# A planned four-layer graph kernel: first batch in halves, first weights on another queue, three batches kept on chip, and a reordered tail

## The chip, the core and the metric

The kernel runs on one core of one Trainium2 chip. The time is the device time of one execution in microseconds (us); where several executions were timed, their median is given. The engines are PE (TensorE, the matrix products), DVE (VectorE), ACT (ScalarE), POOL (GpSimd) and SP (SyncE, which here only issues transfers); "PEld" in the profile is the loading of a product's stationary operand, which lies beside PE's products. The core has 16 DMA engines, which all queues share. One profiled execution gives the trace; all times inside it count from the start of its span.

## What is computed

There are 32 batches; `x` is 32 x 512 x 128, `adj` 32 x 512 x 512, symmetric, of zeros and ones with ones on the diagonal, all float32. Four layers of the form x + f(relu(layernorm(x)), adj) follow each other:

```python
def L0(x, mask):                      # masked attention
    v, q, k = relu(x Wv' + bv), relu(x Wq' + bq), relu(x Wk' + bk)
    h = clip((q k') * mask, 0, 9e13) - 9e15 * (1 - mask)
    return softmax(h, axis=2) @ v
def L1(x, A):                         # A_norm = d^-1/2 (A + I) d^-1/2
    dyn = conv1d(x[:, -128:, :])      # the last 128 rows, kernel width 3
    lw = lstm(dyn)                    # 128 steps, state 32 x 128
    return sigmoid((A_norm @ x) @ lw)
def L2(nodes, adj):                   # four times
    src_agg = l2norm(adj, 2) @ (nodes ws + bs)
    dst_agg = l2norm(adj, 1)' @ (nodes wd + bd)
    return tanh([src_agg, nodes wn + bn, dst_agg] wu + bu)
def L3(clip, adj, W, bias, a):
    g = adj @ (clip W') + bias
    return where(g >= 0, g, a * g)
```

The LSTM of layer 1 runs over the last 128 rows of every batch, and its output enters every row of that batch: nothing behind it can start before its last step.

## The kernel before

The function `symmetric` (L792) computes everything for a symmetric `adj`. It also counts violations into a flag `fail`, and a second program, `general`, runs behind a branch on that flag if it isn't zero. All engines read the flag (`counted`, L1671; `read`) and take the branch at the end.

**Who sets the order.** The code doesn't issue instructions where it names them. Each step is recorded with `plan.op` (helpers `PE`, `ACT`, `DVE`, `POOL`, `DMA`), with its engines, a duration as the planner supposes it, a rank, what it reads and writes, and a `gap` until its result may be used. `Plan.run` (L612) then simulates the engines with these durations, always takes the step that can start first, by rank among equals, and writes the instructions out in that order. A lower rank is more urgent: the LSTM's steps have ranks 0 to 127, loads of the head `HEAD`, pass 1 10,000 and up, pass 2 20,000, the rest 30,000. Two constants say how long a less urgent step may keep an awaited LSTM step from its engine: `HOLD` (L538), and `PATIENCE` (L825) for the products of `fold`. Buffers come from pools of named tags with fixed numbers (`BUFS`: 8 of "x", 5 of "y", 4 each of "n0" to "n3" and "inv", 5 of "xn", 8 PSUM banks "mm"); a step that needs a new buffer waits until the planner sees one free.

**Head.** `load` (L947) issues the attention's weights (`w_att`, 192 KB), the bias columns `colb` and a bias row of V (L954) on SP, behind the two halves of the first batch's x and ahead of the second batch's x. ACT begins with an activation on a scrap tile (L938) that makes it load its table. PE runs 20 products on a constant (`warm_up`, L970). Weights of layer 2 are combined beforehand by `fold` (L1019), four times, placed by `FOLD_AT` behind batches of pass 1.

**Pass 1** (`pass_1`, L1151; 0 to 186 us) takes the batches in order. It loads x (256 KB) and the last 128 columns of adj (`al`), normalises (`ln_full`: statistics L1070 on DVE, a power L1080 on POOL, x-hat L1090 or L1093), transposes and applies relu (`ln_t`, into half 1 of the tile `kh`), computes K (L1168, into half 0 of `kh`), Q for the last 128 rows, and V (L1184), then scores (L1201), exponential (L1205), mask (L1206) and output (L1211) for these rows, and from their new values the convolution's input (L1226, L1236). It stores K and the transposed relu (`dkq`, 448 KB), V (`dv`, 258 KB) and the new last rows (`dl`) in HBM.

**LSTM stage** (186 to 503 us). `lstm` (L1249) runs the 128 steps for all batches at once: products of w with the state (f_z, L1263), tanh (L1289), cell (L1295), state (L1309). Each step is a chain through PE, ACT and DVE, and PE has little of its own to do in it. The gaps are filled with `pass_2` (L1321), the attention of the first 384 rows: it loads `dkq` and `dv` back, the rows of `adj` and x again, and computes Q (L1348), scores (L1357), exponential (L1360), mask and output (L1363, L1367, L1369). Further filler is the early sums of layer 1 (`aggregate`, L1479, with the product at L1483).

**Rest** (`rest`, L1501; 503 us to the end) does layer 1's last product, the four rounds of layer 2 (L1592, L1483, L1599, L1603, L1607) and layer 3 for one batch per turn; the turns overlap. Layer 3 of a turn is: new x (L1622), layer norm, the split of relu into two parts whose sum is used in the product (`relu_parts`, in the last turn `relu_first`, L1461, four 128-column pieces, with ACT's L1472 and DVE's L1474), aggregation (L1636 in the last turn), product with W (L1650), and then three steps for the activation with slope a: the negative part on ACT (L1653), the positive part added on DVE (L1654), and minus a times the negative part (L1656). Then the result is stored. In the last turn (31) the steps from L1636 on come in two halves, and the second half is stored by ACT (L1660). Sixteen products on a constant keep PE at work in the last turn.

## Time and profile before

| what | value |
|---|---|
| median of 3 runs | 1282.03 us (1279.73 to 1284.29) |
| profiled execution | 1284.31 us, its span 1282.4 us |
| granted clock of PE | 1.00 as a mean |
| PE busy | 1255.4 us, 98% of the span |
| DVE, ACT, POOL busy | 982.7, 836.9, 399.3 us |
| moved by DMA | 237.15 MB, 185 GB/s over the span |
| LSTM stage | 186.4 us (first f_z) to 503 us |

A page of the profile gives busy time by engine, the shares of the chain that ended last (followed back from the last instruction to what released it), and groups of instructions by line. Other views are answers of the same trace: waits (who waited for whom: total us, times, longest), stretches (busy time of each engine in a time window), the chain piece by piece in order of time (start, length, what), and a timeline (start, length, engine, line, instruction). Matmuls are pipelined and their ends are modelled, so a PE that is shown as busy need not be at its peak rate.

### The profile page before, as it was taken

How to read it: one execution, taken by the hardware profiler on the slowest of the kernel's cores; microseconds unless marked ns; L12 is line 12 of the kernel's file. 1: busy time of each engine (PE TensorE's matmuls, PEld its weight loads, DVE VectorE, ACT ScalarE, POOL GpSimd, SP SyncE). 2: the span in 40 equal slices, each digit the busy share in tenths (PEclk: the TensorE clock that was granted, in tenths of full speed). 3: DMA queues.
4: the chain of work that ended last, by engine and by line, in shares of the span. 5: the costliest groups of instructions: out<-in, count | busy, mean ns of one | idle time of the engine just before them, and what ended most of it. 6: DMA issues, size and time to landing. Idle time of an engine off the chain costs nothing.

```text
span 1282.4 us, 33056 instructions
## 1 busy us (share of the span) xinstructions
PE 1255.4 (98%) x12073; PEld 970.9 (76%) x12074; DVE 982.7 (77%) x3275; ACT 836.9 (65%) x2099; POOL 399.3 (31%) x734
## 2 busy tenths in 40 slices
PE   9999999999999989999999999999999999999997
PEld 6989876666666667777878778787787787877775
DVE  7798969888989879876667677677676776787745
ACT  5566658777867646776567666676676766675433
POOL 4555533232323224332223224223232242232101
PEclk9999999999999999999999999999999999999999
DMA  8888888887868896778367777777777777473211
GB/s 268 265 264 279 280 272 264 263 267 229 269 201 260 249 245 192 161 179 198 85 151 177 155 164 166 147 176 159 152 180 151 175 151 151 98 163 69 50 25 44
DMA packets 316843, 237.15 MB, mean 185 GB/s; under 512 B 151936, under 2 KB 260736, under 8 KB 316672
## 3 DMA queue, kind: packets, MB, share of 16 engines
q1 hardware_dynamic: 299504, 218.04, 62.3%
q0 software_dynamic: 16896, 16.78, 8.4%
q8 instruction: 97, 1.59, 0.5%
q14 instruction: 74, 0.61, 0.2%
q10 hardware_dynamic: 272, 0.13, 0.0%
HBM read 138.68 MB, written 64.75 MB: 159 GB/s over the span
## 4 chain that ended last, share of the span: by engine, by line
PE 83%; DVE 8%; DMA 2%; ACT 2%; POOL 2%; issue 1%; SPq 0%; ACTq 0%; DVEq 0%
PE f_pa L1483 18%; PE f_py L1592 15%; PE f_pa L1603 15%; PE f_pg L1483 7%; PE f_s L1357 4%; PE f_po L1363 3%; PE f_z L1263 3%; PE f_pk L1168 2%; PE f_pv L1184 2%; PE f_p L1650 2%; PE f_pol L1211 2%; PE f_pl L1557 2%; PE f_sl L1201 2%; PE f_pd L1236 2%; DMA f_a<-in_adj_dram 2%
## 5 line engine op out<-in xcount | busy, mean ns | idle before, releaser
L1483 PE MATMUL f_pa<-f_ar,f_y 128*128 128x512 f32 x1024 | 300.6, 430 | 0.4 <-ACT f_y L1448 0.4
L1483 PEld LDWEIGHTS f_pa<-f_ar,f_y 128*128 128x128 f32 x1024 | 189.3, 188 | 75.8 <-issue 40.4
L1592 PE MATMUL f_py<-f_wf,f_n 128*128 128x128 f32 x1280 | 174.1, 275 | 0.0
L1592 PEld LDWEIGHTS f_py<-f_wf,f_n 128*128 128x128 f32 x1280 | 165.1, 191 | 8.6 <-issue 1.0
L1607 ACT ACTIVATE f_n<-f_pa,f_bcol 128x512 f32<-128x512 f32 x128 | 88.1, 688 | 104.4 <-PE f_pa L1603 101.6
L1603 PE MATMUL f_pa<-f_n,f_wf 128*128 128x512 f32 x320 | 153.1, 593 | 0.2 <-DVE f_pa L1599 0.2
L1403 ACT ACTIVATE f_ar<-f_a 128x512 fp32r<-128x512 f32 x224 | 138.8, 622 | 6.4 <-DMA f_a<-in_adj_dram 4.0
L1410 POOL DMA_DIRECT2D f_das<-f_ar x32 | 27.1, 847 | 365.8 <-ACT f_ar L1403 345.2
L1448 ACT CAST f_y<-f_py 128x512 fp32r<-128x512 f32 x128 | 75.3, 589 | 66.9 <-PE f_py L1592 64.2
L1449 DVE TENSOR_TENSOR f_y<-f_py,f_y 128x512 fp32r<-128x512 f32 x128 | 87.9, 688 | 37.4 <-ACT f_y L1448 36.8
L1599 DVE TENSOR_TENSOR f_pa<-f_pa,f_inv 128x512 f32<-128x512 f32 x128 | 87.0, 695 | 33.5 <-PE f_pa L1483 33.4
L1363 PE MATMUL f_po<-f_v,f_e 128*32 128x129 f32 x3072 | 107.2, 273 | 1.9 <-issue 1.9
L1363 PEld LDWEIGHTS f_po<-f_v,f_e 128*32 128x32 f32 x3072 | 90.1, 110 | 20.3 <-issue 17.1
L1357 PE MATMUL f_s<-f_q,f_k 128*32 128x384 f32 x1024 | 99.0, 487 | 0.2 <-ACT f_e L1360 0.2
L1263 PE MATMUL f_z<-f_w,f_seq 128*32 128x128 f32 x2040 | 83.2, 276 | 11.3 <-DVE f_seq L1309 4.1
L1603 PEld LDWEIGHTS f_pa<-f_n,f_wf 128*128 128x128 f32 x320 | 57.4, 190 | 46.0 <-issue 42.0
L1263 PEld LDWEIGHTS f_z<-f_w,f_seq 128*32 128x32 f32 x2040 | 54.2, 109 | 49.1 <-ACT f_e L1360 11.9
L1121 DVE COPY f_hl_d<-f_n 128x1024 uint16<-128x1024 uint16 x26 | 18.1, 694 | 88.8 <-ACT f_n L1607 88.8
L1419 DVE SCALAR_TENSOR_TENSOR f_aT<-f_a,f_aT 128x1024 bf16<-128x1024 f32 (+1 forms) x68 | 76.3, 1155 | 0.1
L1592 PE MATMUL f_py<-f_wf,f_T_c 128*128 128x128 f32 x448 | 72.9, 275 | 0.0
L1483 PE MATMUL f_pg<-f_ar,f_xp_d 128*128 128x512 f32 x248 | 71.6, 412 | 0.0
L1360 ACT ACTIVATE f_e<-f_s 128x384 f32<-128x384 f32 x128 | 61.1, 484 | 15.2 <-PE f_s L1357 8.5
(208 smaller groups left out, 2751.4 us busy)
## 6 DMA issues: line engine op xcount, KB each, us to landing
f_a<-in_adj_dram SPq DMA_DIRECT2D x112, 256.0 KB
f_a<-in_adj_dram SPq DMA_DIRECT2D x28, 1024.0 KB
f_das<-f_ar POOLq DMA_DIRECT2D x32, 512.0 KB, 4.8
f_dkq<-f_kh SPq DMA_DIRECT2D x32, 448.0 KB
f_dv<-f_v SPq DMA_DIRECT2D x32, 258.0 KB
f_v<-f_dv SPq DMA_DIRECT2D x32, 258.0 KB
f_al<-in_adj_dram SPq DMA_DIRECT2D x32, 256.0 KB
f_k<-f_dkq SPq DMA_DIRECT2D x32, 256.0 KB
```

The costliest lines, as they stand in the source:

```text
L1263: nc.tensor.matmul(z.t[part, k, :, :], h, w[:, m : m + 4, part], start=False, stop=True, skip_group_check=True)
L1357: PE(R, t_mm(NR), lambda s=s, j=j: quarters(lambda p: nc.tensor.matmul(s.t[p], keys.t[:, j * P + p.start : j * P + p.stop], q.t, start=Tru ...
L1363: PE(R, t_mm(P), lambda e=e, t=t, j=j: quarters(lambda p: nc.tensor.matmul(po.t[p, t, :], e.t[:, t * P + p.start : t * P + p.stop], v.t[:, ...
L1403: ACT(rank, 0.62, lambda t=t: nc.scalar.activation(ar.t[:, t, :], a.t[:, t, :], AF.Square, accum_out=deg.t[:, t : t + 1]), [(a, t)], [(ar, ...
L1419: nc.vector.scalar_tensor_tensor(flat(aT.t[:, n * k : n * (k + 1), :]), flat(a.t[:, n * k : n * (k + 1), :]), 1.0, flat(aT.t[:, n * k : n ...
L1448: ACT(rank, t_act(N), lambda: nc.scalar.copy(parts.t[:, :, 0, :], src.t), [src], [(parts, 0)])
L1449: DVE(rank, t_dve(N), lambda: nc.vector.tensor_sub(parts.t[:, :, 1, :], src.t, f32(parts.t[:, :, 0, :])), [src, (parts, 0)], [(parts, 1)])
L1483: nc.tensor.matmul(pg.t, parts.t[:, j, k, :], ar.t[:, j, :], start=(k == 0 and j == 0), stop=(k == 1 and j == NT - 1))
L1592: nc.tensor.matmul(py.t[:, j, :], nodes[n].t[:, bass.ts(j, P)], wf[:, W_F[i] + c, 0, :], start=False, stop=(c == nch - 1), skip_group_chec ...
L1599: before = DVE(R, t_dve(N), lambda pa=pa: nc.vector.tensor_mul(pa.t, pa.t, inv_row.t), [inv_row], [pa])
L1603: nc.tensor.matmul(pa.t, wf[:, W_F[i] + c, 1, :], nodes[n].t, start=False, stop=(c == nch - 1), skip_group_check=True)
L1607: ACT(R, 0.57, lambda pa=pa, n=n, i=i: nc.scalar.activation(n.t, pa.t, AF.Tanh, bias=bcol[:, i : i + 1]), [pa], [n])
```

## The change

It has five parts, and moves the order of the instructions on all engines, since the planner plans everything anew.

1. Planner constants: `HOLD` 0.18 to 0.15, `PATIENCE` 0.9 to 1.3, the folds behind the positions 2, 3, 4, 5 of pass 1 instead of 1, 3, 5, 7. (`LEAD = 0.0` and `Q_FIRST = range(0)` leave branches in the code that do nothing.)
2. The three first weights are issued by ACT (`load_beside`), ahead of its table load.
3. Pass 1 takes batches 3 to 31 first and then 0, 1, 2. The batch at position 0 is handled in two halves of 256 rows up to K, and position 1 has its variance sum on DVE ("quick").
4. Batches 0, 1, 2 (`RESIDENT`) are neither stored after pass 1 nor loaded for pass 2: `kh`, `v` and `xc` stay in their buffers.
5. In the tail, the negative part, its addition and the store of turns 29 and 30 are recorded within `relu_first` of turn 31, behind its fourth piece (`put_off`). In every turn the positive part is recorded ahead of the negative one. The flag is read behind the last store instead of behind the last aggregation.

```diff
--- before.py
+++ after.py
@@ -535,7 +535,7 @@
...
-    HOLD = 0.18
+    HOLD = 0.15
...
-    FOLD_AT = (1, 3, 5, 7)
+    FOLD_AT = (2, 3, 4, 5)
...
+    RESIDENT = range(3)
+    FIRST_GAPS = (2.0, 2.8, 3.0, 3.5)
...
-    PATIENCE = 0.9
+    PATIENCE = 1.3
...
-    nc.scalar.activation(table, neg_half[:, 0, 0:1], AF.Exp)
...
-    w_att = load(HEAD + 0.1, 192, w[:, :W_CONV, :], weights[:, :W_CONV, :])
-    w_cols = load(HEAD + 0.2, 5, colb, cols)
-    DMA(HEAD + 0.3, 64, lambda: nc.sync.dma_start(brow[:, BR_V, :], rows[R_V].partition_broadcast(P)), [], [(biases, BR_V)])
+    def load_beside(dst, src, c, gap):
+        return ACT(HEAD, 0.45, lambda: nc.scalar.dma_start(dst, src), [], [c], gap=gap)
+
+    w_att, w_cols = plan.fixed(w), plan.fixed(colb)
+    load_beside(w[:, :W_CONV, :], weights[:, :W_CONV, :], w_att, 3.5)
+    load_beside(colb, cols, w_cols, 3.0)
+    load_beside(brow[:, BR_V, :], rows[R_V].partition_broadcast(P), (biases, BR_V), 3.0)
+    ACT(HEAD, 1.5, lambda: nc.scalar.activation(table, neg_half[:, 0, 0:1], AF.Exp))
     w_conv = load(HEAD + 12, 192, w[:, W_CONV:W_IH, :], weights[:, W_CONV:W_IH, :])
     w_crow = load(HEAD + 12, 64, conv_row, rows[R_CONV].partition_broadcast(P))
...
-    def pass_1(b):
-        R = 10_000 + b * 10
+    staying = {}
+
+    def pass_1(b, pos):
+        R = 10_000 + pos * 10
         xc = new("x", (P, NT, P), f"f_x_{b}")
-        n = 2 if b == 0 else NT
+        n = 2 if pos == 0 else NT
         for at in range(0, NT, n):
             DMA(R, 64 * n, lambda at=at: nc.sync.dma_start(xc.t[:, at : at + n, :], x[b].rearrange("(t p) d -> p t d", p=P)[:, at : at + n, :]), [],
-                [(xc, t) for t in range(at, at + n)] if b == 0 else [xc], gap=2.0 if b == 0 else 4.5 if b < 4 else 3.5)
+                [(xc, t) for t in range(at, at + n)] if pos == 0 else [xc], gap=FIRST_GAPS[pos] if pos < len(FIRST_GAPS) else 3.5)
         al = new("n1", (P, NT, P), f"f_al_{b}")
         DMA(R + 11, 256, lambda: nc.sync.dma_start(al.t, adj[b, :, NR:].rearrange("(t p) i -> p t i", p=P)), [], [al])
-        xn = ln_full(R, xc, f"a{b}", quick=b == 0)
...
         kh = new("y", (P, 2, N), f"f_kh_{b}")
-        turned = ln_t(R, xn, None, f"a{b}", ((kh, 1), lambda: kh.t[:, 1, :]))
...
+        if pos == 0:
+            hs, ks = [], []
+            xn = new("xn", (P, NT, P), f"f_xn_a{b}")
+            for at in range(0, NT, n):
+                tiles = range(at, at + n)
+                part = slice(at * P, (at + n) * P)
+                mv = ln_stats(R, xc, tiles, f"a{b}_{at}")
+                rs = new("rs", (P, NT), f"f_rs_a{b}_{at}")
+                ln_rstd(R, mv, at, at + n, (lambda rs=rs, at=at: rs.t[:, at : at + n], rs), True)
+                for t in tiles:
+                    DVE(R, t_dve(P), lambda t=t, mv=mv, rs=rs: nc.vector.tensor_scalar(
+                        xn.t[:, t, :], xc.t[:, t, :], mv.t[:, t, 0:1], rs.t[:, t : t + 1], OP.subtract, OP.mult), [(xc, t), mv, rs], [(xn, t)])
+                tp = bank(f"f_xt_a{b}_{at}", (P, n, P), whole=False)
+
+                def turn(tp=tp, tiles=tiles):
+                    for k, t in enumerate(tiles):
+                        nc.tensor.matmul(tp.t[:, k, :], xn.t[:, t, :], ident, start=(k == 0), stop=True, is_transpose=True, skip_group_check=True)
+                turned = PE(R, n * T_TR, turn, [(xn, t) for t in tiles], [tp])
+                hs.append((kh, ("h", at)))
+                ks.append((kh, ("k", at)))
+                evict(R, n * P, lambda part=part: kh.t[:, 1, part], lambda tp=tp: flat(tp.t), [tp], hs[-1:], relu=True)
+                project(R, n * P, W_K, C_K, lambda part=part: kh.t[:, 1, part], lambda part=part: kh.t[:, 0, part], hs[-1:], ks[-1:], f"k_{b}_{at}")
+        else:
+            hs, ks = [(kh, 1)], [(kh, 0)]
+            xn = ln_full(R, xc, f"a{b}", quick=pos == 1)
+            turned = ln_t(R, xn, None, f"a{b}", (hs[0], lambda: kh.t[:, 1, :]))
+            project(R, N, W_K, C_K, lambda: kh.t[:, 1, :], lambda: kh.t[:, 0, :], hs, ks, f"k_{b}")
         ql = new("low", (P, P), f"f_ql_{b}")
-        project(R, N, W_K, C_K, lambda: kh.t[:, 1, :], lambda: kh.t[:, 0, :], [(kh, 1)], [(kh, 0)], f"k_{b}")
-        project(R, P, W_Q, C_Q, lambda: kh.t[:, 1, NR:], lambda: ql.t, [(kh, 1)], [ql], f"ql_{b}")
+        project(R, P, W_Q, C_Q, lambda: kh.t[:, 1, NR:], lambda: ql.t, hs[-1:], [ql], f"ql_{b}")
...
-        PE(R, 4 * t_mm(P), values, [(kh, 1), w_att], [pv])
+        PE(R, 4 * t_mm(P), values, hs + [w_att], [pv])
...
-        DMA(R + 5, 448, lambda: nc.sync.dma_start(dkq.t, flat(kh.t)[:, : N + NR]), [kh], [dkq])
-        DMA(R + 5, 258, lambda: nc.sync.dma_start(dv.t, v.t), [v], [dv])
+        if b in RESIDENT:
+            staying[b] = kh, v, xc
+        else:
+            DMA(R + 5, 448, lambda: nc.sync.dma_start(dkq.t, flat(kh.t)[:, : N + NR]), [kh], [dkq])
+            DMA(R + 5, 258, lambda: nc.sync.dma_start(dv.t, v.t), [v], [dv])
...
-        PE(R, 4 * t_mm(P), scores, [(kh, 0), ql], [s])
+        PE(R, 4 * t_mm(P), scores, ks + [ql], [s])
...
-        keys = new("inv", (P, N), f"f_k2_{b}")
-        hT = new("xn", (P, NR), f"f_h2_{b}")
-        v = new("n3", (P, NT, P + 1), f"f_v2_{b}")
-        xc = new("x", (P, NT if whole else L, P), f"f_x2_{b}")
-        DMA(R, 192, lambda: nc.sync.dma_start(hT.t, dkq.t[:, N:]), [dkq], [hT], gap=LANDED)
-        DMA(R, 256, lambda: nc.sync.dma_start(keys.t, dkq.t[:, :N]), [dkq], [keys], gap=LANDED)
+        stays = b in RESIDENT
+        if stays:
+            kh, v, xc = staying[b]
+            keys, keys_of = kh, lambda: kh.t[:, 0, :]
+            hT, h_of = kh, lambda: kh.t[:, 1, :NR]
+        else:
+            keys = new("inv", (P, N), f"f_k2_{b}")
+            hT = new("xn", (P, NR), f"f_h2_{b}")
+            keys_of, h_of = lambda: keys.t, lambda: hT.t
+            v = new("n3", (P, NT, P + 1), f"f_v2_{b}")
+            xc = new("x", (P, NT if whole else L, P), f"f_x2_{b}")
+            DMA(R, 192, lambda: nc.sync.dma_start(hT.t, dkq.t[:, N:]), [dkq], [hT], gap=LANDED)
+            DMA(R, 256, lambda: nc.sync.dma_start(keys.t, dkq.t[:, :N]), [dkq], [keys], gap=LANDED)
...
-        DMA(R, 258, lambda: nc.sync.dma_start(v.t, dv.t), [dv], [v], gap=LANDED)
-        DMA(R, 192, lambda: nc.sync.dma_start(xc.t[:, :L, :], x[b, :NR].rearrange("(t p) d -> p t d", p=P)), [],
-            [(xc, t) for t in range(L)], gap=LANDED)
-        if whole:
+        if not stays:
+            DMA(R, 258, lambda: nc.sync.dma_start(v.t, dv.t), [dv], [v], gap=LANDED)
+            DMA(R, 192, lambda: nc.sync.dma_start(xc.t[:, :L, :], x[b, :NR].rearrange("(t p) d -> p t d", p=P)), [],
+                [(xc, t) for t in range(L)], gap=LANDED)
+        if whole and not stays:
             DMA(R, 64, lambda: nc.sync.dma_start(xc.t[:, L, :], dl.t), [dl], [(xc, L)], gap=LANDED)
...
+        for finish in put_off:
+            finish(parts.parts[0, NT - 1][0], parts.parts[1, NT - 1][0])
...
+        if turn == B - 1:
+            R += 4
...
-                warm_up(R, 0.216, f"f_warm_{k}_{b}", [end4])
+                warm_up(R - 4, 0.216, f"f_warm_{k}_{b}", [end4])
...
-            late.append(agg3)
...
-            ACT(R, t_act(n * P), lambda p3=p3, part=part: nc.scalar.activation(neg.t[:, part, :], p3.t, AF.Relu, scale=-1.0), [p3], [(neg, at)])
             DVE(R, t_dve(n * P), lambda p3=p3, part=part: nc.vector.scalar_tensor_tensor(
                 flat(xc.t[:, part, :]), flat(p3.t), 0.0, flat(xc.t[:, part, :]), OP.max, OP.add), [p3], mine)
-            DVE(R, 0.15 + 0.125 * n, lambda part=part: nc.vector.scalar_tensor_tensor(
-                flat(xc.t[:, part, :]), flat(neg.t[:, part, :]), minus_alpha, flat(xc.t[:, part, :]), OP.mult, OP.add),
-                [(neg, at), w_alpha], mine)
-            if at:
-                ACT(R, 0.5, lambda part=part: nc.scalar.dma_start(out[b].rearrange("(t p) d -> p t d", p=P)[:, part, :], xc.t[:, part, :]),
-                    mine, [], gap=2.0)
+
+            def finish(turned=(), split=(), at=at, p3=p3, part=part, mine=mine):
+                ACT(R, t_act(n * P), lambda: nc.scalar.activation(neg.t[:, part, :], p3.t, AF.Relu, scale=-1.0), [p3], [(neg, at)], after=turned)
+                DVE(R, 0.15 + 0.125 * n, lambda: nc.vector.scalar_tensor_tensor(
+                    flat(xc.t[:, part, :]), flat(neg.t[:, part, :]), minus_alpha, flat(xc.t[:, part, :]), OP.mult, OP.add),
+                    [(neg, at), w_alpha], mine, after=split)
+
+                def store():
+                    return (nc.scalar if at else nc.sync).dma_start(out[b].rearrange("(t p) d -> p t d", p=P)[:, part, :], xc.t[:, part, :])
+                return ACT(R, 0.5, store, mine, [], gap=0.0) if at else DMA(R, 64 * n, store, mine, [], gap=0.0)
+            if turn in (B - 3, B - 2):
+                put_off.append(finish)
             else:
-                DMA(R, 64 * n, lambda part=part: nc.sync.dma_start(out[b].rearrange("(t p) d -> p t d", p=P)[:, part, :], xc.t[:, part, :]),
-                    mine, [])
+                stored = finish()
+            if turn == B - 1:
+                late.append(stored)
...
-        PE(R, 0.1, read, [], [], after=[said] + late)
+        PE(R + 4, 0.1, read, [], [], after=[said] + late)
...
-    for b in range(B):
-        pass_1(b)
+    for pos, b in enumerate([b for b in range(B) if b not in RESIDENT] + list(RESIDENT)):
+        pass_1(b, pos)
         for i, at in enumerate(FOLD_AT):
-            if at == b:
-                fold(i, 10_000 + b * 10)
+            if at == pos:
+                fold(i, 10_000 + pos * 10)
...
```

## The prediction, made before the changed kernel was run

> **What bounds the kernel now.** The page's first lines and its chain shares say which engine sets the end:
>
> ```profile
> span 1282.4 us, 33056 instructions
> PE 1255.4 (98%) x12073; PEld 970.9 (76%) x12074; DVE 982.7 (77%) x3275; ACT 836.9 (65%) x2099; POOL 399.3 (31%) x734
> PE 83%; DVE 8%; DMA 2%; ACT 2%; POOL 2%; issue 1%; SPq 0%; ACTq 0%; DVEq 0%
> ```
>
> TensorE is idle for only 27 us. The change leaves the products of the computation as they are (one is split in two halves), so those 27 us, and whatever "busy" hides, are all there is. The table by stretches (length, busy time and count of PE, PEld, DVE, ACT, POOL, then clock, DMA share, GB/s) says where:
>
> ```profile
> 200.00:250.00 50.00, 46.80 (x1024) 31.70 (x1020) 43.98 (x182) 37.48 (x134) 15.26 (x28) 1.00 0.85 263
> 400.00:500.00 100.00, 93.12 (x1984) 65.59 (x1980) 85.97 (x359) 64.65 (x229) 31.04 (x56) 1.00 0.89 248
> 550.00:1250.00 700.00, 699.62 (x3768) 546.16 (x3767) 496.63 (x1274) 446.84 (x942) 188.65 (x279) 1.00 0.65 141
> 1250.00:1283.00 33.00, 25.81 (x143) 19.30 (x142) 17.63 (x60) 12.39 (x26) 3.54 (x5) 0.97 0.15 43
> ```
>
> From 550 to 1250 nothing can be won. What can move is the head, the LSTM stage (186 to 503) and the tail. PE's waits, and the LSTM's tanh, whose 128 executions date the steps:
>
> ```profile
> PE f_z L1263 <- DVE f_seq L1309: 4.1, 12, 0.9
> PE f_z L1263 <- issue: 3.0, 3, 2.3
> PE f_pq L1348 <- issue: 2.0, 1, 2.0
> PE f_po L1363 <- issue: 1.9, 2, 1.3
> ```
> ```profile
> L1289 ACT ACTIVATE f_th<-f_z x128: 228/251/259, 187.8 to 502.8; 128x96 f32<-128x96 f32 x128
> ```
>
> (502.8 − 187.8)/127 = 2.48 us a step. The ends of matmuls are modelled, so "busy" hides slack; I priced PE's order by undisturbed pieces of the chain: 1.72/4 = 0.43 us a record of 128x512 (the piece at 1246.83), 1.85/8 = 0.23 for the early sums (1248.55), 2.68/24 = 0.11 for 128x128 (1243.26), and 0.22 for eight of the LSTM's tiled ones (distance of their starts). That makes 276 us of work in the 317 of the LSTM stage, so some 40 of slack; about 10 in pass 1 (20 to 186), 7 from 550 to 1250.
>
> **The LSTM stage.** New: HOLD, PATIENCE, three resident batches. PE's order between two tanh gives each step its work; a step of max(2.17, work + 0.05 + 0.30 for each change to tiled products and back), 2.17 being the shortest steps of the trace, sums to 298.9 us for 126 steps against 313.1 measured. Of the 14.2 above it, 11.2 lie in ten stalled steps. In the changed order the 16 starved steps (under 1.4 us of filler) become 11, and the same sum gives 296.9: −2.0. By the same prices, PE has 1.1 us less to do before the LSTM (170.5 → 169.4) and 0.4 less after it (763.4 → 763.0), the stage itself taking in 1.3 more (276.4 → 277.7): −1.5. Together −3.5 if the chip keeps the planner's timing, 0 if it doesn't; I take −2.8, nearer the first, since the sum already follows the chip's steps to 5% (298.9 against 313.1).
>
> The residents drop 3 × (448 + 258) KB of stores and 3 × (192 + 256 + 258 + 192 + 64) KB of loads, about 5 MB of 237. At the 263 GB/s of the first LSTM stretch that is 19 us of transfer time, but beside PE's work; SP issues 20 instructions fewer. No PE wait above names a load, so the value is bounded by 0 and the 3.5 us of the small waits on masks and scores (rinv 1.5, ar 1.3, el 0.9, all partly load-driven). I take −0.7, near zero, since most name DVE or ACT. What hides the stores today is PE's work; without that cover each 706 KB would cost 2.7 us.
>
> Here a rule speaks. The Trainium skill, "Runtime: NRT & Kernel Launch", section Instruction fetch mechanics, has instruction memory refilled in 16 KiB blocks, with the crossing mostly hidden. The rows differ: the three longest "issue" waits (2.3 at 440.9, 2.0 at 475.1, 1.3 at 208.9; 5.5 us) each stand beside a refill of the instruction queue (from 439.5, 474.7, 207.9). By the rule another order changes nothing there; by the rows up to 5.5 us can go, or come as often again. The changed order has 18 PE rows more in 5,670, so refills are as many and only fall elsewhere; I take 0, with ±3.
>
> The order of batches and the fold's places (1, 3, 5, 7 to 2, 3, 4, 5) are the same instructions in another order; their gaps are in the −1.5 above.
>
> **The head.** SyncE issues, one behind another:
>
> ```profile
> 1.75 0.46 SPq L949 DMA_DIRECT2D f_w<-in_weights_dram  x1
> ...
> 2.73 0.43 SPq L954 DMA_DIRECT2D f_brow<-in_rows_dram  x1
> 3.20 0.43 SPq L1156 DMA_DIRECT2D f_x<-in_x_dram  x1
> ```
>
> The three weights now go out on ScalarE at about 0.74 to 2.1, ahead of the table load (1.28 us), which ends at 3.4 instead of 2.0. Behind it on ScalarE stands the first x-hat at 5.85: 2.2 us of cover. On SyncE the second x goes out at 1.75 instead of 3.20. The fold's first 384 KB move behind it, its mask and three more issues, to about 4.2 from 3.68; they landed at 8.76, so near 9.3, and are first used at 11.4: no cost. The Trainium skill, "DMA: Bandwidth & Descriptors", section Issuing engines are not separate DMA queues, says that all engines' transfers share the same 16 and that a second issuer saves only issue time. By that rule at most 1.45 us, and the weights (192 KB, 0.7 us at the page's 268 GB/s of the first slice) now share the engines with the first x, which can land 0 to 0.5 later. The first chain:
>
> ```profile
> 1.19 6.15 PE f_warm L973 x20
> 7.33 0.45 PE f_xt_a L895 x4
> ...
> 7.81 0.61 ACT f_kh L900
> ...
> 8.46 1.12 PE f_pk L1168 x2
> ...
> 9.80 0.91 PE f_pv L1184 x8
> ...
> 13.36 0.71 PE f_pol L1211 x4
> ```
>
> By halves, each of statistics, power (GpSimd, 1.02 us at 4.60 for four columns) and x-hat starts on its own half of x, so both x-hats are there near 6.5. That wins nothing yet: the 20 warm-up products, counted the same in the changed order, keep PE until 7.17, when the first transpose starts. (They also cover an x that lands 0.5 late.) From there: first half of the relu at 7.6 to 8.0 (half of 0.61, plus overhead), first half of K at 8.0, second at 8.5 to 8.95, where K ended at 9.42: −0.45. Values 9.2 to 10.05, scores from 10.05 to 10.95, which before began at 10.86. Then PE waits for the exponential and the mask: exp 11.1 to 11.6, mask to 12.3. Before, PE idled from 12.25 to 13.36 there. In the changed order the next batch, with its x 1.45 earlier, has its transposes (0.45), the fold's (0.33) and its K product (0.86) ahead of f_pol. Its relu comes on ScalarE behind the exp, 11.7 to 12.3, so K runs 12.3 to 13.2 and f_pol starts at 13.2 with 0.86 more behind it: −1.0. By the rule at most −1.45; by the row of the second x (landed 7.73, near 5 afterwards) I would have counted 2.4. I take −1.0, from −1.4 to +0.3 (DVE is 98% busy from 60 to 80, and may give back what PE wins).
>
> **The tail.** VectorE sets when the last aggregation ends:
>
> ```profile
> 1269.87 0.74 DVE L1656 SCALAR_TENSOR_TENSOR f_x<-f_neg,f_minus_alpha,f_x 128x512 f32<-128x512 f32 x1
> 1271.33 0.87 DVE L1474 SCALAR_TENSOR_TENSOR f_xp_d<-f_yr_d,f_rs_d,f_xp_d 128x128 fp32r<-128x128 f32 x3
> 1272.14 0.75 DVE L1656 SCALAR_TENSOR_TENSOR f_x<-f_neg,f_minus_alpha,f_x 128x512 f32<-128x512 f32 x1
> 1272.81 0.34 DVE L1474 SCALAR_TENSOR_TENSOR f_xp_d<-f_yr_d,f_rs_d,f_xp_d 128x128 fp32r<-128x128 f32 x1
> ```
>
> Both L1656 go behind the fourth part, and on ScalarE the negative part of turn 30 (0.60 at 1271.51) no longer stands before its last x-hat (1272.00): the parts end at about 1272.1 instead of 1273.15, −1.0. The two updates (1.5 us) then run to 1273.6 while PE finishes and warms (1273.9 to 1275.0); uncovered they would give it all back. The stores of turns 29 and 30 start some 1.5 later with them, well ahead of the last one at 1277.8. The final chain: the positive part no longer follows the negative one, −0.4; but the flag read (0.48 on ACT at 1275.49, in the shadow of PE's products) now stands behind the last store's issue, and ACT's branch follows it, +0.5. So 0, from −0.5 to +0.5. Tail: −1.0.
>
> **Sum.** −2.8 − 0.7 + 0 − 1.0 − 1.0 = −5.5. Against the profiled execution: span 1282.4 → 1276.9, and with the 1.9 around it (1284.31 − 1282.4) 1278.8. The median of the runs shown lies 2.3 below that execution: 1282.0 − 5.5 = 1276.5.
>
> **Rivals.** (A) As summed: 1276.5, own range 1273.5 to 1279. (B) The stalled steps were artefacts of this order: half of the 11.2 goes too, about 1271. For it: three of ten are refills, which need not recur. Against: nothing in the change aims at them. (C) The packing doesn't do what it says: steps hang on delays that the planner does not see (4.1 us of PE's waits are on DVE's f_seq), and the 1.3 us of work taken in lengthen the stage. Then 1282.0 − 1.0 − 1.0 − (1.5 − 1.3) = 1279.8. Against: starved steps cost 2.17 whatever they hold. (D) Slower: at the border of the passes the residents hold 3 of 4 buffers "n3" (v) and 3 of 5 "y", so the loads of v for batches 4 to 6 wait for pass 2 of batches 0 to 2. A batch of pass 2 takes 317/32 = 9.9 us, a 256 KB load some 4.5 (x in the head), so one batch of lead suffices; it decides once the loads take over 9.9 us from the freeing, as with DMA at 0.85 busy they might. Then filler is missing for up to two steps a batch: 2 × (2.17 − 0.43 of LSTM products) = 3.5, times three = 10.4, less the 5.5: 1286.9. Two late batches of the three make it slower than before.
>
> **Chances and range.** A 0.50, B 0.20, C 0.20, D 0.10. A measurement of this kernel tells 0.3% (3.9 us) from no change: bounds 1278.2 and 1285.9. Faster: 0.92 of A, all of B, a third of C = 0.73, with a bit of D's low end 0.75; slower: six tenths of D = 0.06; same 0.19. Range 1268.5 (B with all stalls gone but packing halved) to 1282.5 (C with head and tail lost): it leaves out D and a little of B.
>
> **What would show it.** Head: transposes still at 7.2, K's first half near 8.0, scores near 10.1. LSTM: tanh from about 185.6 to 498.5, 2.46 a step; a sum of issue waits near 5 to 7. Border: no PE wait on a v or x load near 185 to 220. Tail: last part of L1527 near 1 us earlier against the n4 transpose, the last branch as far behind the store as before. Wrong if issue waits grow past 10 us, if pass 1 ends no earlier, or if PE waits for v.

## The result and the profile after

The changed kernel took 1276.24 us in the median of ten runs (1274.55 to 1280.98), the kernel before 1283.10 in ten (1279.31 to 1287.63): a ratio of 0.9949, 95% interval 0.9932 to 0.9966, so 6.5 us faster. 5.5 us were forecast. The sum came out nearly right and most of its terms did not, as the traces show. The profiled execution after is one of the shorter ones (span 1273.4, time 1275.34), that of before one of the longer (1284.31); the difference of 9.0 us between those two spans is 2 to 3 us too large. So where I compare stages below I use several traces of the same plan.

The page's first lines and chain shares of the changed kernel:

```profile
span 1273.4 us, 33089 instructions
PE 1255.8 (99%) x12074; PEld 970.9 (76%) x12075; DVE 985.9 (77%) x3275; ACT 837.8 (66%) x2102; POOL 400.7 (31%) x734
PE 86%; DVE 6%; POOL 2%; ACT 2%; DMA 2%; issue 1%; SPq 0%; ACTq 0%; DVEq 0%
```

PE's busy time is the same within 0.4 us; what changed is its idle time, 27 us before and 17.6 after. By stretches (the same columns as before):

```profile
200.00:250.00 50.00, 49.44 (x1088) 34.32 (x1084) 46.49 (x194) 38.35 (x136) 15.37 (x28) 1.00 0.70 218
400.00:500.00 100.00, 97.80 (x1968) 69.69 (x1960) 89.30 (x369) 68.23 (x239) 33.83 (x64) 1.00 0.85 238
550.00:1250.00 700.00, 699.58 (x3763) 545.78 (x3763) 498.08 (x1268) 438.62 (x918) 182.51 (x271) 1.00 0.63 138
```

PE is at work 49.4 us of the first 50 behind 200 (46.8 before) and 97.8 of the 100 from 400 (93.1 before; in the changed kernel the last 8 of them lie behind the LSTM stage); 550 to 1250 has nothing in it, as said. The DMA share at the beginning of the stage fell from 0.85 to 0.70. PE's waits in the stage and the tanh that dates the steps:

```profile
PE f_z L1303 <- DVE f_seq L1349: 2.3, 7, 0.6
PE f_z L1303 <- issue: 0.7, 2, 0.4
PE f_z L1303 <- DVE f_rinv L1419: 0.6, 2, 0.4
PE f_z L1303 <- ACT f_ar L1456: 0.3, 1, 0.3
PE f_s L1409 <- issue: 0.2, 1, 0.2
```
```profile
L1329 ACT ACTIVATE f_th<-f_z x128: 227/251/255, 186.5 to 491.6; 128x96 f32<-128x96 f32 x128
```

Two lines of before that belong beside these:

```profile
PE f_z L1263 <- DVE f_rinv L1367: 1.5, 3, 1.0
PE f_z L1263 <- ACT f_ar L1403: 1.3, 3, 0.7
```

Issue waits (those for which the profile names no other engine) fell from 6.9 us to 0.9 in this trace, and the waits on the filler's f_rinv and f_ar from 2.8 to 0.9. The stage, from the first tanh to the last, fell from 315.0 to 305.1 us.

### The profile page after: what moved, and what is told of

Same layout as the page of the kernel before. It is cut to its first block, busy times and chain, and to the rows that moved or that the text cites. A ratio compares the mean times of both kernels' runs of the same rounds, so it can differ in the third digit from the quotient of the medians.

```text
span 1273.4 us, 33089 instructions
## 1 busy us (share of the span) xinstructions
PE 1255.8 (99%) x12074; PEld 970.9 (76%) x12075; DVE 985.9 (77%) x3275; ACT 837.8 (66%) x2102; POOL 400.7 (31%) x734
## 4 chain that ended last, share of the span: by engine, by line
PE 86%; DVE 6%; POOL 2%; ACT 2%; DMA 2%; issue 1%; SPq 0%; ACTq 0%; DVEq 0%
PE f_pa L1538 18%; PE f_py L1647 15%; PE f_pa L1658 15%; PE f_pg L1538 8%; PE f_po L1415 5%; PE f_z L1303 4%; PE f_s L1409 4%; PE f_pol L1251 2%; PE f_pk L1177 2%; PE f_p L1706 2%; PE f_sl L1241 2%; PE f_pv L1219 2%; PE f_pl L1612 2%; PE f_pd L1276 2%; PE f_pq L1399 1%; DVE f_e L1413 1%
## 5 line engine op out<-in xcount | busy, mean ns | idle before, releaser
L1409 PE MATMUL f_s<-f_q,f_k 128*32 128x384 f32 x928 | 92.0, 486 | 0.2 <-issue 0.2
L1538 PE MATMUL f_pg<-f_ar,f_xp_c 128*128 128x512 f32 x256 | 68.4, 407 | 0.6 <-ACT f_xp_c L1509 0.4
```

What stands on the lines that cost most here:

```text
L1409: PE(R, t_mm(NR), lambda s=s, j=j: quarters(lambda p: nc.tensor.matmul(s.t[p], keys_of()[:, j * P + p.start : j * P + p.stop], q_of(), sta ...
L1538: nc.tensor.matmul(pg.t, parts.t[:, j, k, :], ar.t[:, j, :], start=(k == 0 and j == 0), stop=(k == 1 and j == NT - 1))
```

## The experiments

Every experiment is a kernel of its own. "Ratio" is its time over that of the kernel before, run beside it, with the 95% interval in brackets; the change itself has 0.9949. Work is PE's priced work as in the prediction (without warm-up products), and slack is a stage's length less its work; for slack, the LSTM stage runs from the first product f_z to the last. "Change" means the changed kernel.

### 1. The kernel before, once more

Edit: none. A second trace.

> The kernel before, unchanged, for a second trace of it. Question: are the stalls of its LSTM stage (ten steps with 11.2 us over what their work takes, three of them issue waits of 5.5 us in all) bound to this order of instructions, or accidents of one execution? Bound to the order: the longest steps are again 104 (4.93 us), 117 (4.62), 82, 78, the stage lasts 315 us within 1.5, issue waits of PE within it are 6 to 8 us. Accidents: other steps are long, the issue waits come to anything from 0 to 7 us, the stage lasts 307 to 313 us.

One execution: time 1284.62 us, stage 314.1. Of the twelve longest steps eight are the same as in the first trace, step 117 with 4.62 us in both; but step 104 (4.93) is gone. Its four issue waits sum to 4.0 us; the first trace has six with 6.9. So both answers hold in part: about half of the stalls sit at fixed places of this order, the others come and go from execution to execution.

### 2. The flag read behind the last aggregation again

```diff
             evict(R, n * P, lambda cols=cols: g3.t[:, cols], ...)
+            late.append(agg3)
-            if turn == B - 1:
-                late.append(stored)
-        PE(R + 4, 0.1, read, [], [], after=[said] + late)
+        PE(R, 0.1, read, [], [], after=[said] + late)
```

> The changed kernel with one part undone: the flag is read behind the last aggregation, as before, not behind the last store. Theory: in the changed kernel PE's branch (4.68 us, from 1266.51) ends at 1271.24 and SyncE's closing waits hang on it, so the end lies 6.5 us behind the issue of the last store, against 4.6 before; with the early read PE's branch starts some 2 us earlier and the last store's landing (2.6 us) sets the end again: 1.5 to 1.9 us faster than the changed kernel, so about 1274.5 us. Rival: ACT's branch stands behind the last store anyhow and its code takes 3 us to come, so the end stays 6 us behind the store and the flag reads on DVE and ACT delay the last halves by 0.3: no gain, 1276 to 1277 us.

1276.61 us, ratio 0.9964 (0.9952 to 0.9976): no gain over the change. The end lies 6.1 us behind the last store's issue instead of 6.55. The edit moved PE's read only to 1.13 us ahead of the store (0.95 in the change, 3.3 before), so it tests little. It gave something else: the same order of the LSTM stage as the change, with a stage of 307.8 us instead of 305.1, and a step 126 of 4.07 us. Run 8 has that long step again (4.11); the traces of the change and of run 9, in the same order, don't.

### 3. No resident batches

```diff
-    RESIDENT = range(3)
+    RESIDENT = range(0)
```

> The changed kernel without resident batches (RESIDENT = range(0)): batches in the order 0 to 31, all stored and loaded again; everything else as in the change. Theory of packing: PE's order, priced by the same sum as in the prediction, has 165.5 us of work before the LSTM, 295.2 us of steps and 765.3 us behind it, against 165.1, 296.9 and 759.6 in the changed kernel: 4.4 us slower, about 1280.6 us, all of it behind the LSTM. Theory of transfers: the 5 MB cost or relieve waits at the border of the passes: PE busy in 200 to 250 falls from 49.4 us back towards 46.8, and the stage gets 2 to 3 us longer instead of 1.7 shorter. Rival: the residents are worth nothing: 1276 us within 1.

1285.12 us, ratio 1.0026 (1.0016 to 1.0036): about 10 us slower than the change, twice the 4.4 of the order's sum. Its stage takes in 6.2 us less work (271.5 against 277.7), and its first 24 steps have 7.0 us of slack against 4.8. The rest of the loss lies behind the LSTM, where this plan has 16.0 us of slack up to 1250 instead of 10.7. At the border of the passes PE is at work nearly as long as in the change (49.44 us), with the DMA engines busier than in the kernel before (share 0.85, PE 46.80):

```profile
200.00:250.00 50.00, 48.72 (x1012) 33.66 (x1008) 43.00 (x177) 39.64 (x145) 16.24 (x32) 1.00 0.89 279
```

### 4. The planner's old constants in the changed kernel

```diff
-    HOLD = 0.15
+    HOLD = 0.18
-    PATIENCE = 1.3
+    PATIENCE = 0.9
-    FOLD_AT = (2, 3, 4, 5)
+    FOLD_AT = (1, 3, 5, 7)
```

> The changed kernel with the planner's constants of before (HOLD 0.18, PATIENCE 0.9, folds behind positions 1, 3, 5, 7). Theory of packing: by the same sum 166.6 + 295.8 + 767.2 us against 165.1 + 296.9 + 759.6 in the changed kernel: 8 us slower, 1284 us, mostly because 9 us less of work fits into the LSTM stage. Rival (the planner's timing is not the chip's; the constants only shuffle): 1276 us within 1.5.

1294.08 us, ratio 1.0092 (1.0067 to 1.0117): 18 us slower than the change. Its waits of PE in the stage:

```profile
PE f_z L1303 <- DVE f_seq L1349: 12.7, 24, 1.7
```

The stage holds 9 us less work and still lasts 311.2 us: 45.0 us of slack. The waits on the LSTM's state (f_seq) are 12.7 us, against 2.3 to 5.1 in five traces of the change's order.

### 5. The new constants alone in the kernel before

```diff
-    HOLD = 0.18
+    HOLD = 0.15
-    PATIENCE = 0.9
+    PATIENCE = 1.3
-    FOLD_AT = (1, 3, 5, 7)
+    FOLD_AT = (2, 3, 4, 5)
```

This is the reverse of edit 4, in the kernel before.

> The kernel before with one part of the change alone: the planner's constants (HOLD 0.15, PATIENCE 1.3, folds behind batches 2, 3, 4, 5). Theory of packing, the order's sum alone: 164.7 + 298.8 + 760.5 us against 166.2 + 298.9 + 759.9 before: 1.0 us faster, 1281.5 us, and the LSTM stage keeps some 39 us of slack. Theory of stalls: the traces so far show 14 us above the modelled steps with the old constants and 5 to 6 with the new ones; if the constants are what removes the stalls, the stage gets 8 us shorter here too, 1273 to 1275 us, and PE's waits on the LSTM's state (f_seq) and issue waits fall below 4 us together.

1281.93 us, ratio 0.9996 (0.9984 to 1.0007): no gain that can be told from nothing, where the order's sum had 1.0 us; the theory that the constants as such remove the stalls falls. The stage does get shorter (310.7 us, 34.6 of slack), but 2.4 us more slack than in the kernel before lie in the first 60 us behind it.

### 6. HOLD alone undone

```diff
-    HOLD = 0.15
+    HOLD = 0.18
```

> The changed kernel with one constant undone: HOLD 0.18, so that a filler may keep an LSTM step waiting 0.03 us longer in the plan. By the order's sum: 165.1 + 307.1 + 751.6 us against 165.1 + 296.9 + 759.6: a longer stage with 8 us more work in it, 2.2 us slower than the change in all, 1278.5 us. Theory of stalls: if it is HOLD that lets fillers collide with the LSTM on the chip, the steps are some 14 us above the modelled ones instead of 6, and the time is 1286 us with waits on f_seq above 4 us. If HOLD is not the cause: 6 above the model, 1278.5 us.

1283.11 us, ratio 1.0011 (0.9999 to 1.0022). The stage takes in 8 us more work, with 30.1 us of slack, just as the change; waits on f_seq are 2.4. So HOLD doesn't cause the stalls. What is lost is lost behind the LSTM: 8.9 us of slack in its first 60 us, 3.4 in the change. A stage that is filled more takes filler away that would have covered the start of the rest.

### 7. The first weights on SyncE again

```diff
-    load_beside(w[:, :W_CONV, :], weights[:, :W_CONV, :], w_att, 3.5)
...
+    nc.scalar.activation(table, neg_half[:, 0, 0:1], AF.Exp)
+    w_att = load(HEAD + 0.1, 192, w[:, :W_CONV, :], weights[:, :W_CONV, :])
+    w_cols = load(HEAD + 0.2, 5, colb, cols)
+    DMA(HEAD + 0.3, 64, lambda: nc.sync.dma_start(brow[:, BR_V, :], ...))
```

> The changed kernel with the first weights issued by SyncE again, ahead of the second x, and ACT's table load first. Theory (the weights on ACT's queue share the DMA engines with the first x, which landed at 4.18 instead of 3.02): the first statistics start at 3.0 again. But PE's first transpose comes at 7.17 either way, behind the warm-up products, and the wait in the head of the changed kernel is another: the scores (11.71 instead of 10.86) wait for K, whose second half waits on DVE behind the statistics of the third x (landed 10.67). So scores before 11 and PE's lag at 20 us below 10.2 if the third x is issued as late as before; by the order's sum 167.5 + 294.9 + 761.7 us against 165.1 + 296.9 + 759.6: 2.5 us slower, 1278.5 us. Rival: issuing on ACT itself is worth the 1.45 us of issue time and the head loses it: scores at 12 or later.

1284.31 us, ratio 1.0017 (1.0007 to 1.0026). The first statistics start at 2.96 us again, the scores at 11.2; but slack before the LSTM is 24.3 us instead of 20.0, of which 2.6 us more lie between 20 and 60 us, where the plan is another one. So the loss of this plan isn't what the head alone gains by ACT's queue; the other queue makes another plan.

### 8. The flag read under the warm-up products

```diff
-        R = 30_000 + (B - 1) * 10
+        R = 30_000 + (B - 4) * 10
...
-                late.append(stored)
+            late.append(end4)
-        PE(R + 4, 0.1, read, [], [], after=[said] + late)
+        PE(30_000 + (B - 1) * 10, 0.5, read, [], [], after=[said] + late)
```

> The changed kernel with the violations counted some turns earlier and the flag read by all engines while PE runs its warm-up products behind the last transpose, instead of behind the last store; nothing else. The run with the read behind the last aggregation moved PE's read by only 0.2 us against the store (1.13 ahead of it instead of 0.95), so it didn't test the tail. Theory: the code behind the branch takes PE 4.5 us to come, ACT 3 us; PE can now branch right behind its last product (1.5 us earlier) and ACT right behind the last store (0.5 earlier), so the end lies 5.3 to 5.6 us behind the last store's issue instead of 6.55: 1.0 us faster than the change, 1275.3 us. Rival: the last store's own landing or SyncE's closing waits set the end: no gain.

1278.01 us, ratio 0.9959 (0.9943 to 0.9975); the end is 5.9 us behind the store's issue instead of 6.55, and the time can't be told from that of the change. All engines read the flag 8 to 10 us ahead of the store, and PE's instructions behind the branch still come 4.2 us after it, SyncE's 3.3. But PE's branch itself moved only to 0.50 us ahead of the store (0.36 in the change): warm-up products that wait for ACT's f_neg stand in front of it. So neither run 2 nor run 8 tests an early branch of PE. That the last store's own landing sets the end, the rival, is what the traces show (see the tail below).

### 9. The updates of turns 29 and 30 in their own place

```diff
-            if turn in (B - 3, B - 2):
+            if turn in ():
```

> The changed kernel with one part of the tail undone: negative part, its addition and the store of turns 29 and 30 come in their own turns again, ahead of the last turn's pieces on ACT and DVE; the order of PE's instructions is the same. Theory: the way from the last turn's new x to the issue of its last store, 11.07 us before and 10.28 in the change, is 11.1 again: 0.8 to 1.0 us slower than the change, 1277.2 us. Rival (DVE has room there, the gain comes from the positive part going first): 10.3 again, no difference.

1277.40 us, ratio 0.9953 (0.9936 to 0.9969): no difference. DVE's timeline and the chain in this kernel:

```profile
1263.43 1.13 DVE L1527 SCALAR_TENSOR_TENSOR f_xp_d<-f_yr_d,f_rs_d,f_xp_d 128x128 fp32r<-128x128 f32 x4
1264.55 0.74 DVE L1714 SCALAR_TENSOR_TENSOR f_x<-f_neg,f_minus_alpha,f_x 128x512 f32<-128x512 f32 x1
```
```profile
1264.10 1.18 PE f_pg L1693 x10
```

The last pieces end 6.14 us behind the new x (at 1258.42), in the change 5.50; but PE's last aggregation ends 6.86 us behind it in both (1265.28 here). In the change, where the pieces come earlier, they find PE still at the products and warm-ups ahead of theirs.

### 10. The saved traffic put back

The batches 26 to 31 store K, relu and V twice; PE's order is that of the change, instruction by instruction.

```diff
+            def keep(b=b, dkq=dkq, kh=kh):
+                if b >= B - 6:
+                    nc.sync.dma_start(dkq2, flat(kh.t)[:, : N + NR])
+                return nc.sync.dma_start(dkq.t, flat(kh.t)[:, : N + NR])
...
+            DMA(R + 5, 448, keep, [kh], [dkq])
```

> The changed kernel with the saved traffic put back without changing the plan: the batches 26 to 31 store K, relu and V twice (6 x 706 KB = 4.2 MB more, beside 5 MB that the resident batches save), the second copy to a place nobody reads. The order of PE is the same. Theory of packing (the residents' worth is that their pass 2 can start at once, not the bytes): 1276.3 us within 1. Theory of transfers: the border of the passes (160 to 250 us) gets 1 to 3 us longer, PE busy in 200 to 250 falls below 48.5, and the time is 1278 to 1280 us.

1283.73 us, ratio 1.0005 (0.9989 to 1.0022): 7 us slower with the same plan. The stretch 140 to 180 of the change, and then of this kernel:

```profile
140.00:180.00 40.00, 39.80 (x326) 34.07 (x328) 31.12 (x120) 29.47 (x71) 19.18 (x50) 1.00 0.82 270
```
```profile
140.00:180.00 40.00, 35.40 (x255) 30.01 (x254) 26.66 (x108) 24.07 (x54) 16.05 (x45) 0.96 1.01 333
```

and this kernel's longest waits of PE in pass 1:

```profile
PE f_pd L1289 <- DVE f_mv_a L1083: 2.7, 1, 2.7
PE f_pd L1289 <- DVE f_sh_a L1112: 1.9, 1, 1.9
```

The DMA engines are full (1.01), and transfers land late. A store of V, issued at 141.73, takes 6.4 us (2.8 to 4.9 in the change), and its buffer stays taken so long: GpSimd waits for it, its powers for the layer norm come late, and PE waits 1.9 us. On SyncE the next x stands behind two more stores of V, one of them an added one, so it is issued at 149.07 (146.16 in the change), and it takes 7.35 us to land (3.5 in the change); its statistics hold VectorE, and PE waits 2.7 us.

```profile
148.24 0.10 POOL L1212 MEMSET f_v<- 128x4 f32 x1 [3.23 <-DMA f_dv<-f_v]
```
```profile
149.07 7.35 DMA f_x<-in_x_dram
```

These two waits are 4.6 us. Another 1.6, by estimate, are the granted clock, 0.96 over these 40 us in this trace (0.66 from 160 to 165) and 1.00 in the change.

The LSTM starts at 191.5 instead of 185.1; the stage (308.0) and all behind it are as in the change. At the border, 200 to 250, where the theory of transfers had its loss, PE is at work 49.45 us, as in the change. The kernel before carries a higher share than 0.82 in pass 1 without a loss:

```profile
140.00:160.00 20.00, 19.96 (x156) 16.93 (x155) 18.00 (x81) 13.65 (x29) 9.77 (x25) 1.00 0.89 285
```

So the room that is left there is less than these 4.2 MB in some 40 us, while a share of 0.89 did no harm. The added stores take issue time on SyncE as well as transfer time, and this run doesn't separate the two. The change takes 2.1 MB of stores out of the last 20 us of pass 1; that it gained in pass 1 by this is not shown (slack before the LSTM 20.0 after, 20.2 before).

### 11 and 12. Refills moved by half a block

The K products of pass 1 are split in two of 256 columns, in the kernel before and in the changed one. Work and plan stay; 4 more PE records per batch, 128 in all, move every later refill of PE's instruction memory by half a block (the first trace has 97 refills for 24,504 records of PE, one for some 253).

```diff
-            PE(rank, t_mm(n), lambda: nc.tensor.matmul(pq.t, w[:, m, :], src(), start=True, stop=True), r + [w_att], [pq])
+            def both():
+                for at in range(0, n, 256 if n == N else n):
+                    cut = slice(at, at + (256 if n == N else n))
+                    nc.tensor.matmul(pq.t[:, cut], w[:, m, :], src()[:, cut], start=at == 0, ...)
+            PE(rank, t_mm(n), both, r + [w_att], [pq])
```

> The kernel before, with each K product of pass 1 (512 columns) split into two of 256: the same work and the same plan, but 4 more PE instructions for each of 32 batches, so that from the LSTM stage on every refill of PE's instruction memory falls 128 instructions, half a block, earlier in the program. Theory of refills: the gap of 2.44 us at f_pq near 475 us, step 117, which both traces of the kernel before show with a refill at its start, goes or moves to another place; other gaps appear elsewhere, and the stage stays within 311 to 316 us. Rival (the gap belongs to that place in the program, not to the refill): it stays at step 117 with some 2.4 us.

> The changed kernel with the same split of the K products (29 to 31 of them, first batch aside), so refills about half a block earlier in the LSTM stage; work and plan are those of the changed kernel. Theory: the changed kernel's stage (305.1, 307.8 and 308.5 us in three traces of the same order) owes up to 3 us to where its refills happen to fall; with the shift it lies at 306 to 311 us and the time at 1276 to 1279 us. If refills don't matter for it: 1276.3 us within 0.7 and the gap of 2.2 us near step 126, seen in two of the three traces, in the same place.

Shifted before: 1286.89 us, ratio 1.0022 (1.0008 to 1.0037). Shifted change: 1278.62 us, ratio 0.9961 (0.9943 to 0.9980), stage 306.3 us, and the gap near step 126 isn't in it; but two of four traces without the shift don't have it either. The place of step 117 in PE's timeline, before (first trace), before (second trace) and shifted:

```profile
477.09 1.13 PE L1348 MATMUL f_pq<-f_h,f_w 128*32 128x384 f32 x9 [1.95 <-issue]
```
```profile
477.47 1.13 PE L1348 MATMUL f_pq<-f_h,f_w 128*32 128x384 f32 x9 [1.95 <-issue]
```
```profile
470.74 1.50 PE L1352 MATMUL f_pq<-f_h,f_w 128*32 128x384 f32 x16
```

Twice a group of 16 is cut after the seventh for the same 1.95 us, at a refill; with the refills half a block away it runs through. The count of PE's records says the same: the cut stands at a place that comes back every 256 records, and the two other long issue waits of the first trace stand at that place too (see the last section). So this stall belongs to the refill. But the time isn't won: four steps later, in step 121, the shifted kernel waits where neither trace of before did,

```profile
PE f_pq L1352 <- DMA f_h<-f_dkq: 2.8, 1, 2.8
```

on a load issued at 477.7 that lands at 483.5, 5.8 us later, where the planner counts on 3.3. Its stage is 311.4 us in the trace.

## Why the prediction was right, and where it was wrong

**The total came out by luck.** Before the discount for the planner's timing, the terms of the sum were −2.1 up to the LSTM (moved work and head), −2.7 in the stage (with the transfers), −0.4 behind it and −1.0 in the tail. The table below gives −1.7, −6.2, +1.2 and +0.7: the stage gave 3.5 us more than was summed, and the other three 3.7 less.

Slack by stage in us, from three traces of the plan of before (1, 11 and the first) and five of the plan of the change (the first, 2, 8, 9 and 12):

| | before | changed | work |
|---|---|---|---|
| up to the first LSTM product | 20.2, 21.2, 20.8 | 20.0, 19.9, 20.4, 19.8, 20.5 | 166.2 to 165.1 |
| LSTM stage | 39.1, 38.6, 35.4 | 28.5, 31.0, 31.8, 30.1, 29.6 | 276.4 to 277.7 |
| of it steps 1 to 24 | 8.1, 7.9, 6.7 | 4.8, 4.6, 4.8, 5.1, 4.9 | |
| steps 25 to 60 | 7.8, 9.4, 8.4 | 8.1, 8.6, 8.1, 7.9, 7.5 | |
| steps 61 to 96 | 9.7, 10.6, 10.0 | 7.5, 7.5, 9.1, 7.4, 8.8 | |
| steps 97 to 127 | 13.5, 10.7, 10.4 | 8.2, 10.2, 9.9, 9.7, 8.5 | |
| 60 us behind it | 2.9, 2.9, 2.9 | 3.4, 4.6, 3.7, 3.4, 4.6 | 759.9 to 759.6 |
| from there to 1250 | 6.8, 6.9, 7.9 | 7.3, 7.7, 7.8, 7.9, 8.0 | |
| last new x to last store (length) | 11.07, 11.06, 11.05 | 10.28, 10.45, 10.25, 10.28, 10.28 | |
| last store to end (length) | 4.64, 4.57, 5.15 | 6.55, 6.10, 5.89, 6.52, 6.14 | |

By means, with the work: before the LSTM −0.6 − 1.1 = −1.7; the stage −7.5 + 1.3 = −6.2; behind it −0.3 + 1.0 + 0.5 = +1.2; the tail −0.8 + 1.5 = +0.7. Together −6.0; the spans of these traces differ by 6.2 in the mean, the medians by 6.5.

**The LSTM stage** is the term that was mis-sized: −2.0 by the sum, and −0.7 for the transfers, against −6.2. The packing is there: the sum of the steps' work held in direction. The sum leaves out stalls, and I set their change to 0 with ±3. Gaps of over 0.75 us between the starts of PE's products and weight loads within the stage sum to 13.4, 10.9 and 8.1 us in the three traces before and to 3.3, 6.5, 8.7, 5.0 and 4.6 in the five after (the first, runs 2, 8, 9 and 12): 5.2 us less in the mean, of the 7.5 of slack. So rival B, that about half of the stalls would go, was right for the stage; its total of 1271 was not, since head, rest and tail gave less than it took over from the sum.

What kind of wait went can be read from PE's waits in the same traces. In the mean, issue waits went from 3.8 to 1.9 us, waits on the LSTM's state (f_seq) from 4.2 to 3.1, and all others, f_rinv and f_ar above all, from 4.7 to 1.5: together from 12.7 to 6.4. Run 11 shows that one issue wait was a refill at a bad place. The rule that a crossing is mostly hidden, weighed in the prediction, holds for some 47 of the 50 refills in this stage of the first trace and not for this one: 1.95 us at the same place in two traces, gone with a shift of half a block. But refills are the smaller part of the gain; the larger is that the new order keeps PE less often waiting for the other engines' results.

The first 24 steps have 3 us less slack. The residents, whose pass 2 need not wait for loads, could be the reason, since without them (run 3) these steps have 7.0. But run 5, with the new constants and no residents, has about 5, and run 4, with residents and the old constants, about 9. So bytes, residents and order can't be separated here, and the cause stays open.

**The transfers**, −0.7, can't be told from the rest of the stage. That no wait of PE named a load was no proof of room: run 10 puts 4.2 MB more into the same plan and its trace loses 6.4 us before the LSTM. Nor was the share of 0.85 at the border what kept PE waiting there: without residents (run 3) it is 0.89, and PE is at work 48.72 us of the 50 instead of 46.80.

**The head** failed. The sum had −1.0; the lag of PE at 20 us (its time less the work done) is 9.9 to 10.4 before and 9.3 to 10.3 after, hardly a gain. Two steps of it failed. The first x shares the DMA engines with ACT's weights and came 1.0 to 1.2 us later, not 0 to 0.5: its statistics start at 4.0 to 4.2 where ACT issues the weights and at 3.0 where SyncE does (run 7). And K was evicted late:

```profile
10.70 0.48 DVE L1081 BATCH_NORM_STATS2 f_st_a<-f_x 128x6 f32<-128x128 f32 x2 [1.17 <-DMA f_x<-in_x_dram]
11.10 0.47 DVE L1180 TENSOR_SCALAR f_kh<-f_pk,f_colb 128x256 f32<-128x256 f32 x1
```
```profile
11.71 1.14 PE f_sl L1241 x8
```

The second half of K, finished on PE by 9.4, waits on VectorE behind statistics of the third x. This x was issued at 4.39 and landed at 10.67; the plan had counted on 3.0 us. So the scores began at 11.7 in this trace (11.0 to 12.1 in the five) instead of 10.05. The same reading, who stands behind a waiting instruction, would have shown it in the order of DVE's instructions; I had followed only PE's. The 1.7 us won before the LSTM are the 1.1 of moved work and 0.6 of slack, which remain of some 2 us that pass 1 is ahead at 100 us.

**The tail** failed in two places. Its pieces on DVE did end 0.9 us earlier against the new x (5.50 us, 6.43 before), but PE's last aggregation only 0.3 earlier; run 9 shows that putting off the updates is worth nothing, since PE's own products are the limit there. The final chain gained 0.5 as predicted, by the positive part going first:

```profile
1265.03 0.87 DVE L1709 SCALAR_TENSOR_TENSOR f_x<-f_p,f_x 128x256 f32<-128x256 f32 x2 [1.11 <-PE f_p L1706]
1265.90 0.93 DVE L1714 SCALAR_TENSOR_TENSOR f_x<-f_neg,f_minus_alpha,f_x 128x256 f32<-128x256 f32 x2
```

The flag read I priced at 0 from ACT's branch alone. The way from the last store to the end grew by 1.5 us, and it is the store's own landing that grew. SyncE, the last engine at the end, waits there for that landing, and in 11 of the 14 traces (the table's and those of the other runs) the end lies 2.1 us behind it. What changed in front of it is PE's branch: it stood 2.7 us ahead of the store's issue and now stands 0.4 ahead. From 1.0 to 1.5 us behind the branch, 16 KB of PE's code that follows are fetched. That fetch used to be over when the store was issued; now it runs beside the store. Times in us from the issue of the last store:

| | PE's fetch | last part of the store landed | SyncE behind its branch | end |
|---|---|---|---|---|
| before (first trace) | −1.69 to −0.38 | 2.57 | 0.49 | 4.64 |
| change | 0.67 to 2.99 | 4.48 | 2.97 | 6.55 |
| run 8 | 0.82 to 2.22 | 3.82 | 3.28 | 5.90 |
| run 12 | 0.68 to 2.07 | 3.61 | 3.38 | 6.14 |
| run 3 | 0.69 to 3.09 | 4.58 | 0.49 | 6.69 |
| run 10 | 0.67 to 3.31 | 4.76 | 0.49 | 6.60 |

Runs 3 and 10 rule out SyncE's own late start behind its branch as the cause: there it is as short as before, and the end is as late as in the change. In all ten traces in which PE branches that late the last part lands 1.4 to 1.9 us behind the end of PE's fetch. That the fetch holds up this part is read from this order in time; no run moves PE's branch alone. I had looked at one of five engines that all read the flag.

**The rest.** I took 0.4 us less work behind the LSTM for a gain; slack took it back (+1.5). Run 6 shows the exchange in the large: its stage takes in 8 us more work, and 5.5 us more slack lie in the 60 us behind it.

**The parts don't add.** Taken back one at a time, residents, constants, HOLD or the weights' queue each lose all of the gain, and mostly more (ratios 1.0011 to 1.0092), and the constants alone give none of it (0.9996). Each makes another plan. The order's sum told the sign each time and too small a size: against the change 2.2 to 8.0 us were summed for these plans and for that of before, and 6 to 18 measured. The plan of the change is better than its sum.

## What to carry to other kernels

In a kernel whose order a planner writes, a change's worth is that of the new order: price that order on every engine and queue, not only on the one that is busy, and then doubt the places where a wait stands in front of other work. That no engine waits for a load doesn't say how many more bytes would fit; here 4.2 MB more in 40 us, on a DMA share of 0.82, did not. And a branch fetches code: look at what else is being transferred when it does. Compare stages over several traces of the same order: here single executions differ by 3 us in the stage that the change was to help.

## What the runs showed of the hardware

**Refills of PE's instruction memory.** A stall of 1.95 us repeated to the hundredth in two executions at one refill and went when the program was shifted by half a block. The refills' own transfers were as many and as long in the kernel before and in the change (50 in the stage, 1.16 and 1.14 us in the mean), so the length of the transfer doesn't tell which of them stalls. The place does. I number PE's records (products, weight loads and its semaphore instructions) in the order of the trace and look at gaps of over 1 us between its products and weight loads in the LSTM stage. Of 39 such gaps in the fourteen traces, 14 stand in front of a record whose number is 193 beyond a multiple of 256, and no other place has more than two. In these 14, PE goes on 1.2 to 1.6 us after a refill has ended. The three long issue waits of the first trace, which the prediction lists, are among them, and the shifted kernel before has none. At most three of some 50 refills in a stage stall this long; why these come late is open.

**A fetch beside a store.** The last part of the last store landed 2.5 to 3.1 us behind the issue where PE's fetch behind the branch was over by then (four traces), and 3.5 to 4.8 us behind it where the fetch ran at the same time (ten traces).

**The branch of SyncE.** Behind the branch at the end, SyncE goes on after 0.49 us in six traces (the four of the kernel before and its variants, and runs 3 and 10) and after 2.5 to 3.4 us in the other eight, whether its flag was read 0.5 or 10 us ahead. What decides it is open. It adds some 0.5 us to the end in two traces (runs 6 and 12), where the landing was over before; in the others the landing came later.
